# Tile pools that wait for their own bytes: reuse_waits="tile" on every SBUF and PSUM pool of a four-layer kernel

## The chip, the cores and the metric

The kernel runs on one core of one Trainium2 chip, as one launch. The metric is the device time in microseconds (us). Engines are named as in the profile: PE (matmul; PEld is its weight load), DVE (vector), ACT (scalar), POOL (GpSimd), SP (a queue that only issues DMAs here). A "q" after an engine's name, as in SPq, marks its instruction queue where DMAs are issued.

## The reference: what is computed

The input x is an image of 256 by 256 pixels with 128 channels, fp32. Four layers follow, each with a residual sum and each ahead with a group norm `gn` over 32 groups of channels:

```python
x = x + L0(gn(x))   # attention along the rows, 4 heads of 32, pair bias from x, sigmoid gate, projection
x = x + L1(gn(x))   # a, b = sigmoid((xWa1+ba1)*(xWa2+ba2)), ...; z = einsum('bikc,bkjc->bijc', a, b), 16 channels
                    # g * (LN(z) @ Wz + bz), g = sigmoid(x @ Wg + bg)
x = x + L2(gn(x))   # z = LN(x); a, b = sigmoid(z@Wg)*(z@Wl); k = einsum('bimc,bmjc->bijc', a, b), 128 channels
                    # sigmoid(z@Wgo+bgo) * (LN(k) @ Wlo + blo)
x = x + L3(gn(x))   # a 1x9 convolution to one channel with relu, added down the rows, twice;
                    # then a 1x1 product with relu, added along the columns, twice
```

A group norm needs the mean and variance of the whole image before the next layer can use any pixel. That is why the kernel is a chain of stages with a full statistic between most of them.

## The kernel before, in words

The image is held as 128 channels on the partitions by 65536 pixels. A slab is 2048 pixels (8 KB on each partition, 1 MB in all); there are 32. The image does not fit in SBUF, so each stage streams slabs from DRAM and stores slabs back: xT is the image before layer 0 in that layout, x1T, x2T and x3T are the images after layers 0, 1 and 2.

Stages, with the names of their tile pools and the time of each in the profiled span:

- **p0, p1** (0 to 246 us): load, transpose, statistics of the input; then row factors and pair bias.
- **p2** (246 to 1488): attention, in 64 groups of 4 image rows. The pools are `p2e` (the exponentials, e and es), `p2c` and `p2`. Per group SP loads x and the row factors; ACT centres (L509); PE projects and scores; the reciprocal sums rz go to DRAM and come back spread as rb (L618, L621), POOL multiplies (L636), PE projects (L643), DVE adds to x, and x is stored to x1T (L651). The last two groups store through ACT's queue.
- **chk**: a check that the scores stayed in range, from the statistics `gn_mv` (L799 to L809): chk_ok, a matmul, chk_bad, flag. The flag is read into registers and a conditional block (L811) computes the attention another way if it is set; it isn't in this run. After the block come the norm's factors (L199 to L210) and folded weights (L834 to L842).
- **p3** (1509 to 1582): 13 slab slots, each a pool of its own (`x1_0` to `x1_12`, 8 KB each). The first eight loads (L794 in `load1`) stand in the program ahead of the check. Products a and b go to DRAM (abD).
- **z** (1586 to 1650): the product over k for 16 channels, its norm, result to znD.
- **p4** (1645 to 1817): for each slab a gate on PE and ACT (L987, L990), z's product (L1014), DVE multiplies, POOL adds to x (L1035; DVE does it for six slabs), ACT sums squares (L997), SP stores the slab to x2T (L1041, last L1046), and SP loads later slabs into free slots. Small loads of z are issued by POOL (L973).
- **p5** (1825 to 2347): reads x2T into seven slab buffers (pool `x57`). The first four loads are issued by POOL, the others by SP (L1113). Column sums on PE (L1131) give mean and variance; ACT squares the mean into p5_m2 (L1137); then five products for each slab (L1174), and a and b to DRAM (aD, bD, L1224). The gates of the last two slabs come last.
- **p6** (2351 to 2643): 128 channel products; SP loads A and B (L1278, L1280), PE transposes (L1927) and multiplies (L1938); sums for the norm in k1 (DVE) and k2 (POOL).
- **p7** (2645 to 2916): normalises k, product, gate, residual, store to x3T.
- **p9** (2922 to 3281): layer 3: tap sums on PE (L1509), stored (L1521) and reloaded by image row, then the later relu steps and the output. It begins with a memset on POOL of the tile p9_S (L1695) and slab loads L1325, some of them on POOL's queue.

Memory is a stack of pools: a pool opened after another was released lands on the same bytes. In bytes per partition: the slots x1_0 to x1_12 stand at 48128 to 154624, and before them `p2e` at 48128 to 117760, `p2c` to 128000 and `p2` to 224256. The check's pool starts at 154624, `x57` at 40672, `p5` at 114400, p6 at 128736, p9 at 98016. PSUM is reused in the same way in its eight banks.

What sets the order of the work: within a block under `tc.manual_schedule()` (p0, p1, p2, p3, z, p4, p5, p6, p7 and p9 have one) every engine runs the instructions in the order in which the program gives them. Where such a block's instructions fall among those of its engine outside the block or in the next one is left to the library's planner, which reckons from when inputs and buffers are free. Each engine then runs its list strictly in order, and an instruction that waits holds those behind it. DMAs stand in the list of the engine that issues them.

Of the kernel before, what the change touches and what calls it, by code (L numbers as in the profile page):

```python
# [14 lines left out]
PSUM = bass.MemoryType.PSUM  # L15
# [17 lines left out]
def kernel(ctx: ExitStack, tc: tile.TileContext, a: dict, out: bass.AP):  # L33
# [36 lines left out]

    const = ctx.enter_context(tc.tile_pool(name="const", bufs=1))

# [120 lines left out]
    def gn_groups(mv, name):  # L193

        with tc.tile_pool(name=name + "_ps", bufs=1, space=PSUM) as ps, tc.tile_pool(
            name=name + "_sb", bufs=1
        ) as sb:
            pm = ps.tile([P, 1], F32, name=name + "_pm")
            nc.tensor.matmul(pm, lhsT=gmat, rhs=mv[:, 0:1], start=True, stop=True)  # L199
            mean = const.tile([P, 1], F32, name=name + "_mean")  # L200
            nc.vector.tensor_copy(mean, pm)
            d = sb.tile([P, 1], F32, name=name + "_d")
            nc.vector.tensor_sub(d, mv[:, 0:1], mean)
            nc.vector.scalar_tensor_tensor(d, d, d, mv[:, 1:2], ALU.mult, ALU.add)
            pv = ps.tile([P, 1], F32, name=name + "_pv")
            nc.tensor.matmul(pv, lhsT=gmat, rhs=d, start=True, stop=True)
            sd = sb.tile([P, 1], F32, name=name + "_sd")
            nc.scalar.activation(sd, pv, AF.Sqrt, bias=epst)
            rstd = const.tile([P, 1], F32, name=name + "_rstd")
            nc.vector.reciprocal(rstd, sd)  # L210
        return mean, rstd

    stats_pool = ctx.enter_context(tc.tile_pool(name="stats", bufs=2))

# [11 lines left out]
    layer0 = ExitStack()  # L226
    l0 = layer0.enter_context(tc.tile_pool(name="l0", bufs=1))
    mbT = l0.tile([P, 2, N], F32, name="mbT")
# [9 lines left out]
    RES = NSC // 2 + 2  # L238
    with tc.tile_pool(name="x0", bufs=1) as xres, tc.tile_pool(name="p0", bufs=3) as sb:
        held = {s: xres.tile([P, SC], F32, name=f"x0_{s}") for s in range(RES, NSC)}  # L240
        with tc.tile_pool(name="p0ps", bufs=3, space=PSUM) as ps, tc.tile_pool(
            name="f0ps", bufs=2, space=PSUM
        ) as fps, tc.tile_pool(name="f0", bufs=1) as wk, tc.manual_schedule():
            xts, loaded = {}, {}
# [164 lines left out]

        with tc.tile_pool(name="p1", bufs=2) as wk_sb, tc.tile_pool(  # L410
            name="p1ps", bufs=4, space=PSUM
        ) as ps, tc.tile_pool(name="p1pe", bufs=1, space=PSUM) as psE:

# [67 lines left out]
    qscale = 1.0 / float(HC) ** 0.5  # L481
    with tc.tile_pool(name="p2e", bufs=6) as eb, tc.tile_pool(name="p2c", bufs=1) as cs:
        triT = cs.tile([P, NH, 2, N], F32, name="triT")
        with tc.tile_pool(name="p2", bufs=2) as sb, tc.tile_pool(
            name="p2S", bufs=2, space=PSUM
        ) as psS, tc.tile_pool(name="p2z", bufs=1, space=PSUM) as psZ, tc.tile_pool(
            name="p2M", bufs=3, space=PSUM
        ) as psM, ExitStack() as by_hand:
            groups = {}
# [297 lines left out]
    SLOTS, FIRST = 13, 8  # L787
    x1_scope = ExitStack()
    slots = [x1_scope.enter_context(tc.tile_pool(name=f"x1_{i}", bufs=1)) for i in range(SLOTS)]
    xs = {}  # L790
# [10 lines left out]
    flag = const.tile([P, 1], mybir.dt.int32, name="flag")  # L801
    with tc.tile_pool(name="chk", bufs=1) as sb, tc.tile_pool(name="chkps", bufs=1, space=PSUM) as ps:
        ok = sb.tile([P, 2], F32, name="chk_ok")
        nc.vector.tensor_scalar(ok, mv1, 0.0, 0.0, ALU.mult, ALU.is_equal)
# [4 lines left out]
        nc.vector.tensor_tensor(flag, bad[:, 0:1], bad[:, 1:2], ALU.max)  # L809
# [21 lines left out]
    bgf = const.tile([P, 1], F32, name="bgf")  # L831
    with tc.tile_pool(name="f1ps", bufs=1, space=PSUM) as ps:
# [9 lines left out]
        nc.vector.tensor_tensor(bgf, bg1, pb, ALU.subtract)  # L842
# [6 lines left out]
    with x1_scope:  # L849
        with tc.tile_pool(name="p3", bufs=3) as sb, tc.tile_pool(  # L850
            name="p3ps", bufs=3, space=PSUM
        ) as ps, tc.manual_schedule():
            halves, done = [], []
# [37 lines left out]

        gate_pool = x1_scope.enter_context(tc.tile_pool(name="zg", bufs=3))
        with tc.tile_pool(name="z", bufs=2) as sb, tc.tile_pool(
            name="zps", bufs=3, space=PSUM
        ) as ps, tc.manual_schedule():
            Z = [gate_pool.tile([P, 4, 2 * N], F32, name="z_Z", tag="Z", bufs=4) for _ in range(4)]
# [201 lines left out]
    rs2_scope = ExitStack()  # L1098
    rs2_pool = rs2_scope.enter_context(tc.tile_pool(name="rs2", bufs=1))
# [3 lines left out]
    with tc.tile_pool(name="p5", bufs=2) as sb, tc.tile_pool(  # L1103
        name="p5q", bufs=4
    ) as sq_pool, tc.tile_pool(name="p5psX", bufs=1, space=PSUM) as psX, tc.tile_pool(
        name="p5psM", bufs=3, space=PSUM
    ) as psM, tc.manual_schedule():
        xs, sqs, zns, vars_ = {}, {}, {}, {}
# [691 lines left out]
def general_attention(tc, d, w, dram, stats1):  # L1800
# [6 lines left out]
    statD = dram.tile([N // G, P, 12], F32, name="statD")  # L1807
    with tc.tile_pool(name="gac", bufs=1) as cs, tc.tile_pool(name="ga", bufs=1) as sb, tc.tile_pool(
        name="gae", bufs=2
    ) as eb, tc.tile_pool(name="gaS", bufs=2, space=PSUM) as psS, tc.tile_pool(  # L1810
        name="gaT", bufs=2, space=PSUM
    ) as psT, tc.tile_pool(name="gaM", bufs=2, space=PSUM) as psM:
        tri = cs.tile([P, NH, 2, N], F32, name="ga_tri")
# [166 lines left out]
```

## Time and profile before

| | us |
|---|---|
| time, median of 3 runs | 3282.24 (3282.18 to 3283.38) |
| the profiled execution's own time | 3283.08 |
| its span | 3281.4 |
| PE busy | 3043.8 (93%) |
| DVE busy | 2246.1 (68%) |
| ACT busy | 2034.3 (62%) |
| POOL busy | 1773.0 (54%) |
| mean granted clock of PE | 0.963 |

By stage, busy PE: 1148.0 of 1148 us from 287 to 1435 (p2), 59.9 of 81 from 1509 to 1590 (p3), 137.3 of 140 from 1655 to 1795 (p4), 27.5 of 55 from 1795 to 1850 (p4 to p5), 484.9 of 487 from 1850 to 2337 (p5), 288.6 of 289 from 2354 to 2643 (p6), 247.1 of 248 from 2663 to 2911 (p7), 8.7 of 22 from 2911 to 2933 (p7 to p9).

A line of the timeline reads: start, busy time, engine, line of the program, operation, out<-in, shape, count, and in brackets the idle time of the engine before it and what ended that. A row of waits reads: who waited, for whom, us in total, times, longest. A row of the windows reads: the stretch, its length, busy us (count) of PE, PEld, DVE, ACT and POOL, granted clock, DMA share, GB/s.

### The profile page before, as it was taken

How to read it: one execution, taken by the hardware profiler on the slowest of the kernel's cores; microseconds unless marked ns; L12 is line 12 of the kernel's file. 1: busy time of each engine (PE TensorE's matmuls, PEld its weight loads, DVE VectorE, ACT ScalarE, POOL GpSimd, SP SyncE). 2: the span in 40 equal slices, each digit the busy share in tenths (PEclk: the TensorE clock that was granted, in tenths of full speed). 3: DMA queues.
4: the chain of work that ended last, by engine and by line, in shares of the span. 5: the costliest groups of instructions: out<-in, count | busy, mean ns of one | idle time of the engine just before them, and what ended most of it. 6: DMA issues, size and time to landing. Idle time of an engine off the chain costs nothing. (4 is left out here: it accounts for less than half of the span.)

```text
span 3281.4 us, 51765 instructions
## 1 busy us (share of the span) xinstructions
PE 3043.8 (93%) x19792; PEld 1631.1 (50%) x19792; DVE 2246.1 (68%) x2540; ACT 2034.3 (62%) x2270; POOL 1773.0 (54%) x1019
## 2 busy tenths in 40 slices
PE   5678999999999999996699699999999999979998
PEld 4524555555555555552433244444599943324444
DVE  5626888888888888883456445445455578868887
ACT  3576777777777777763467545444344457757776
POOL 4054777777777777770267100000155568858887
PEclk8898999999999999998999799999999999989999
DMA  9982333333333333329679667766699989986775
GB/s 355 368 325 90 119 117 107 122 111 111 118 111 113 120 107 121 114 88 394 232 299 398 264 232 302 290 226 264 245 351 351 353 321 389 388 304 193 233 232 153
DMA packets 294802, 749.18 MB, mean 228 GB/s; under 512 B 71127, under 2 KB 142185, under 8 KB 245369
## 3 DMA queue, kind: packets, MB, share of 16 engines
q1 hardware_dynamic: 282671, 731.12, 61.2%
q0 software_dynamic: 9040, 13.17, 1.2%
q8 instruction: 158, 2.59, 0.3%
q10 hardware_dynamic: 2840, 1.54, 0.2%
q14 instruction: 93, 0.76, 0.1%
HBM read 458.07 MB, written 287.64 MB: 227 GB/s over the span
## 5 line engine op out<-in xcount | busy, mean ns | idle before, releaser
L565 DVE TENSOR_TENSOR p_e<-p_S,triT 128x1024 f32<-128x1024 f32 x512 | 609.4, 1212 | 145.0 <-PE p_S L555 145.0
L575 POOL TENSOR_TENSOR p_es<-p_e 128x1024 f32<-128x1024 f32 x256 | 603.5, 2369 | 126.9 <-issue 66.1
L573 ACT ACTIVATE p_e<-p_e,mbT 128x1024 f32<-128x1024 f32 x512 | 551.9, 1138 | 62.9 <-DVE p_e L565 62.9
L1174 PE MATMUL p_pm<-p_zn,wf 128*128 128x512 f32 x1040 | 449.0, 593 | 2.1 <-ACT p_a L1209 1.9
L540 PE MATMUL p_mm<-p_xn,w 128*128 128x512 f32 x768 | 407.0, 613 | 0.3 <-DVE p_v L535 0.3
L1174 PEld LDWEIGHTS p_pm<-p_zn,wf 128*128 128x128 f32 x1040 | 197.1, 190 | 254.0 <-issue 246.4
L555 PE MATMUL p_S<-p_q,p_k 32*128 32x256 f32 x4096 | 296.4, 402 | 3.2 <-DVE p_e L565 3.2
L1271 POOL MEMSET k<- 128x512 f32 x1 | 0.5, 524 | 529.4 <-PE p_pm L1174 529.4
L555 PEld LDWEIGHTS p_S<-p_q,p_k 32*128 32x128 f32 x4096 | 186.7, 185 | 159.2 <-PE p_mm L531 91.6
L514 POOL TENSOR_TENSOR p_xn<-p_xn,p_rs 128x1024 f32<-128x1024 f32 x63 | 151.0, 2396 | 207.4 <-ACT p_xn L509 134.2
L1938 PE MATMUL tp_z<-p_B,tp_at 128*128 128x256 f32 x1024 | 250.7, 388 | 0.8 <-DMA p_B<-bD 0.5
L588 PE MATMUL p_o<-p_e,p_v 128*32 128x256 f32 x4096 | 249.3, 384 | 0.0
L1302 POOL TENSOR_TENSOR k<-k,p_sq 128x512 f32<-128x512 f32 x128 | 163.0, 1274 | 135.4 <-ACT p_sq L1300 135.4
L1938 PEld LDWEIGHTS tp_z<-p_B,tp_at 128*128 128x128 f32 x1024 | 185.5, 191 | 22.1 <-DVE tp_at L1929 1.6
L540 PEld LDWEIGHTS p_mm<-p_xn,w 128*128 128x128 f32 x768 | 126.8, 192 | 105.3 <-issue 89.6
L1301 DVE TENSOR_TENSOR k<-tp_z,k 128x512 f32<-128x512 f32 x128 | 88.6, 692 | 127.1 <-ACT p_sq L1300 127.1
L588 PEld LDWEIGHTS p_o<-p_e,p_v 128*32 128x32 f32 x4096 | 120.7, 110 | 110.1 <-ACT p_g L546 41.3
L1298 ACT COPY p_K<-tp_z 128x512 f32<-128x512 f32 x128 | 74.9, 585 | 157.7 <-PE tp_z L1938 157.7
L546 ACT ACTIVATE p_g<-p_mm,bgh 128x512 f32<-128x512 f32 x128 | 88.0, 687 | 131.4 <-PE p_mm L540 131.3
L1213 DVE SCALAR_TENSOR_TENSOR p_b<-p_pm,b2w,p_b 128x1024 f32<-128x1024 f32 x64 | 82.2, 1284 | 123.3 <-PE p_pm L1174 108.9
L544 ACT ACTIVATE p_k<-p_mm,cqkg 128x512 f32<-128x512 f32 x128 | 87.9, 687 | 125.2 <-PE p_mm L540 124.9
L531 PEld LDWEIGHTS p_mm<-w,p_xn 128*128 128x128 f32 x1024 | 134.4, 192 | 61.0 <-issue 60.5
(386 smaller groups left out, 6097.0 us busy)
## 6 DMA issues: line engine op xcount, KB each, us to landing
p_x<-x2T SPq DMA_DIRECT2D x60, 1024.0 KB
x<-x1T SPq DMA_DIRECT2D x51, 1024.0 KB
p_x<-in_x_dram SPq DMA_DIRECT2D x32, 1024.0 KB
p_x<-xT SPq DMA_DIRECT2D x64, 512.0 KB
x2T<-x SPq DMA_DIRECT2D x32, 1024.0 KB
aD<-p_a SPq DMA_DIRECT2D x32, 1024.0 KB
bD<-p_b SPq DMA_DIRECT2D x32, 1024.0 KB
p_A<-aD SPq DMA_DIRECT2D x32, 1024.0 KB
```

The costliest lines, as they stand in the source:

```text
L514: nc.gpsimd.tensor_tensor(xn, xn, groups[g]["rs"], ALU.mult)
L531: nc.tensor.matmul(pm[:, k * D : (k + 1) * D], lhsT=t["xn"][:, b * P : (b + 1) * P], rhs=wf[:, 2 * D : 3 * D], start=True, stop=True,)
L540: nc.tensor.matmul(pm, lhsT=w, rhs=t["xn"][:, cs_], start=True, stop=True)
L555: nc.tensor.matmul(Ss[h // 2][:, h % 2, u, :], lhsT=t["k"][hp, r * N + u * P : r * N + (u + 1) * P], rhs=t["q"][hp, r * N : (r + 1) * N], ...
L565: nc.vector.tensor_tensor(e[:, :, 2 * p : 2 * p + 2, :].rearrange("p u h n -> p h u n"), Ss[p], triT[:, 2 * p : 2 * p + 2, :, :], ALU.add,)
L573: nc.scalar.activation(e[:, u, :, :], e[:, u, :, :], AF.Exp, bias=mbT[:, u, i : i + 1])
L575: nc.gpsimd.tensor_tensor(es, e[:, 0, :, :], e[:, 1, :, :], ALU.add)
L588: nc.tensor.matmul(t["o"][hp, r % 2, :], lhsT=t["v"][:, r * 2 + u, hp], rhs=e[:, u, h, :], start=(u == 0), stop=(u == 1),)
L1174: nc.tensor.matmul(pm[:, c, :], lhsT=wf2[:, i, :], rhs=zns[s][:, k * CK : (k + 1) * CK], start=True, stop=True)
L1301: nc.vector.tensor_tensor(k1, pz, k1, ALU.add)
L1302: nc.gpsimd.tensor_tensor(k2, k2, sq, ALU.add)
L1938: nc.tensor.matmul(pz[:, t, :], lhsT=at[:, u, t * P : (t + 1) * P], rhs=Bc[:, u, :], start=(u == 0), stop=(u == 1))
```

## The change

Each `tc.tile_pool(...)` in SBUF and PSUM gets the argument `reuse_waits="tile"`. Nothing else differs: the same tiles, instructions and transfers, in the same program. The argument tells the library what a tile must wait for when its pool lies on bytes that released pools used. With the default, `"pool"`, every tile of the new pool waits for all users of all those older pools. With `"tile"`, a tile waits for the users of those older tiles that lie on its own bytes (in PSUM, in its own bank). Where the library can't follow an older pool's users it keeps the default for that pool. The waits are made by the library, so no line of the program shows them. A cut of the diff, which repeats for all pools:

```diff
-    with tc.tile_pool(name="p2e", bufs=6) as eb, tc.tile_pool(name="p2c", bufs=1) as cs:
+    with tc.tile_pool(name="p2e", bufs=6, reuse_waits="tile") as eb, tc.tile_pool(name="p2c", bufs=1, reuse_waits="tile") as cs:
...
-    slots = [x1_scope.enter_context(tc.tile_pool(name=f"x1_{i}", bufs=1)) for i in range(SLOTS)]
+    slots = [x1_scope.enter_context(tc.tile_pool(name=f"x1_{i}", bufs=1, reuse_waits="tile")) for i in range(SLOTS)]
...
-    with tc.tile_pool(name="chk", bufs=1) as sb, tc.tile_pool(name="chkps", bufs=1, space=PSUM) as ps:
+    with tc.tile_pool(name="chk", bufs=1, reuse_waits="tile") as sb, tc.tile_pool(name="chkps", bufs=1, space=PSUM, reuse_waits="tile") as ps:
...
-    x_pool = x_scope.enter_context(tc.tile_pool(name="x57", bufs=7))
+    x_pool = x_scope.enter_context(tc.tile_pool(name="x57", bufs=7, reuse_waits="tile"))
...
-    with tc.tile_pool(name="p6", bufs=3) as sb, tc.tile_pool(name="p6ps", bufs=3, space=PSUM) as ps:
+    with tc.tile_pool(name="p6", bufs=3, reuse_waits="tile") as sb, tc.tile_pool(name="p6ps", bufs=3, space=PSUM, reuse_waits="tile") as ps:
```

More of the change, by code (lines that the diff above doesn't have):

```diff
@@ L69 @@
     eD = dram.tile([1, N * NP], F32, name="eD")
-    const = ctx.enter_context(tc.tile_pool(name="const", bufs=1))
+    const = ctx.enter_context(tc.tile_pool(name="const", bufs=1, reuse_waits="tile"))
     ident = const.tile([P, P], F32, name="ident")
@@ L193, in gn_groups @@
     def gn_groups(mv, name):
-        with tc.tile_pool(name=name + "_ps", bufs=1, space=PSUM) as ps, tc.tile_pool(
-            name=name + "_sb", bufs=1
-        ) as sb:
+        with tc.tile_pool(name=name + "_ps", bufs=1, space=PSUM, reuse_waits="tile") as ps, tc.tile_pool(name=name + "_sb", bufs=1, reuse_waits="tile") as sb:
             pm = ps.tile([P, 1], F32, name=name + "_pm")
@@ L211, in gn_groups @@
         return mean, rstd
-    stats_pool = ctx.enter_context(tc.tile_pool(name="stats", bufs=2))
+    stats_pool = ctx.enter_context(tc.tile_pool(name="stats", bufs=2, reuse_waits="tile"))
     def new_stats(name):
@@ L226 @@
     layer0 = ExitStack()
-    l0 = layer0.enter_context(tc.tile_pool(name="l0", bufs=1))
+    l0 = layer0.enter_context(tc.tile_pool(name="l0", bufs=1, reuse_waits="tile"))
     mbT = l0.tile([P, 2, N], F32, name="mbT")
@@ L238 @@
     RES = NSC // 2 + 2
-    with tc.tile_pool(name="x0", bufs=1) as xres, tc.tile_pool(name="p0", bufs=3) as sb:
+    with tc.tile_pool(name="x0", bufs=1, reuse_waits="tile") as xres, tc.tile_pool(name="p0", bufs=3, reuse_waits="tile") as sb:
         held = {s: xres.tile([P, SC], F32, name=f"x0_{s}") for s in range(RES, NSC)}
-        with tc.tile_pool(name="p0ps", bufs=3, space=PSUM) as ps, tc.tile_pool(
-            name="f0ps", bufs=2, space=PSUM
-        ) as fps, tc.tile_pool(name="f0", bufs=1) as wk, tc.manual_schedule():
+        with tc.tile_pool(name="p0ps", bufs=3, space=PSUM, reuse_waits="tile") as ps, tc.tile_pool(name="f0ps", bufs=2, space=PSUM, reuse_waits="tile") as fps, tc.tile_pool(name="f0", bufs=1, reuse_waits="tile") as wk, tc.manual_schedule():
             xts, loaded = {}, {}
@@ L407 @@
         nc.vector.tensor_scalar(woh, wo, 0.5 * SHIFT, None, ALU.mult)
-        with tc.tile_pool(name="p1", bufs=2) as wk_sb, tc.tile_pool(
-            name="p1ps", bufs=4, space=PSUM
-        ) as ps, tc.tile_pool(name="p1pe", bufs=1, space=PSUM) as psE:
+        with tc.tile_pool(name="p1", bufs=2, reuse_waits="tile") as wk_sb, tc.tile_pool(name="p1ps", bufs=4, space=PSUM, reuse_waits="tile") as ps, tc.tile_pool(name="p1pe", bufs=1, space=PSUM, reuse_waits="tile") as psE:
             mw = wk_sb.tile([P, 32], F32, name="p1_mw", bufs=1)
@@ L481 @@
     qscale = 1.0 / float(HC) ** 0.5
-    with tc.tile_pool(name="p2e", bufs=6) as eb, tc.tile_pool(name="p2c", bufs=1) as cs:
+    with tc.tile_pool(name="p2e", bufs=6, reuse_waits="tile") as eb, tc.tile_pool(name="p2c", bufs=1, reuse_waits="tile") as cs:
         triT = cs.tile([P, NH, 2, N], F32, name="triT")
[L484 to L488, printed above, removed]
+        with tc.tile_pool(name="p2", bufs=2, reuse_waits="tile") as sb, tc.tile_pool(name="p2S", bufs=2, space=PSUM, reuse_waits="tile") as psS, tc.tile_pool(name="p2z", bufs=1, space=PSUM, reuse_waits="tile") as psZ, tc.tile_pool(name="p2M", bufs=3, space=PSUM, reuse_waits="tile") as psM, ExitStack() as by_hand:
             groups = {}
@@ L831 @@
     bgf = const.tile([P, 1], F32, name="bgf")
-    with tc.tile_pool(name="f1ps", bufs=1, space=PSUM) as ps:
+    with tc.tile_pool(name="f1ps", bufs=1, space=PSUM, reuse_waits="tile") as ps:
         for w, wf_, ub, vb, n in ((u1, v1, ub1, vb1, "1"), (u2, v2, ub2, vb2, "2")):
@@ L849 @@
     with x1_scope:
-        with tc.tile_pool(name="p3", bufs=3) as sb, tc.tile_pool(
-            name="p3ps", bufs=3, space=PSUM
-        ) as ps, tc.manual_schedule():
+        with tc.tile_pool(name="p3", bufs=3, reuse_waits="tile") as sb, tc.tile_pool(name="p3ps", bufs=3, space=PSUM, reuse_waits="tile") as ps, tc.manual_schedule():
             halves, done = [], []
@@ L888 @@
                 store3()
[L892 to L895, printed above, removed]
+        gate_pool = x1_scope.enter_context(tc.tile_pool(name="zg", bufs=3, reuse_waits="tile"))
+        with tc.tile_pool(name="z", bufs=2, reuse_waits="tile") as sb, tc.tile_pool(name="zps", bufs=3, space=PSUM, reuse_waits="tile") as ps, tc.manual_schedule():
             Z = [gate_pool.tile([P, 4, 2 * N], F32, name="z_Z", tag="Z", bufs=4) for _ in range(4)]
@@ L955 @@
                 nc.sync.dma_start(znD[4 * q : 4 * q + 4, :].rearrange("c (p t) -> p c t", p=P), zq)
-        with tc.tile_pool(name="p4", bufs=3) as sb, tc.tile_pool(
-            name="p4psg", bufs=2, space=PSUM
-        ) as psg, tc.tile_pool(name="p4psz", bufs=2, space=PSUM) as psz, tc.manual_schedule():
+        with tc.tile_pool(name="p4", bufs=3, reuse_waits="tile") as sb, tc.tile_pool(name="p4psg", bufs=2, space=PSUM, reuse_waits="tile") as psg, tc.tile_pool(name="p4psz", bufs=2, space=PSUM, reuse_waits="tile") as psz, tc.manual_schedule():
             zs, gts, sums = {}, {}, []
@@ L1072 @@
     off2 = const.tile([P, 1], F32, name="off2")
-    with tc.tile_pool(name="f2", bufs=1) as sb, tc.tile_pool(name="f2ps", bufs=1, space=PSUM) as ps:
+    with tc.tile_pool(name="f2", bufs=1, reuse_waits="tile") as sb, tc.tile_pool(name="f2ps", bufs=1, space=PSUM, reuse_waits="tile") as ps:
         po = ps.tile([P, 1], F32, name="f2_o")
@@ L1098 @@
     rs2_scope = ExitStack()
-    rs2_pool = rs2_scope.enter_context(tc.tile_pool(name="rs2", bufs=1))
+    rs2_pool = rs2_scope.enter_context(tc.tile_pool(name="rs2", bufs=1, reuse_waits="tile"))
     gates = {s: rs2_pool.tile([P, SC], F32, name=f"gate_{s}") for s in (NSC - 2, NSC - 1)}
@@ L1102 @@
     BT = KB * SC
[L1103 to L1107, printed above, removed]
+    with tc.tile_pool(name="p5", bufs=2, reuse_waits="tile") as sb, tc.tile_pool(name="p5q", bufs=4, reuse_waits="tile") as sq_pool, tc.tile_pool(name="p5psX", bufs=1, space=PSUM, reuse_waits="tile") as psX, tc.tile_pool(name="p5psM", bufs=3, space=PSUM, reuse_waits="tile") as psM, tc.manual_schedule():
         xs, sqs, zns, vars_ = {}, {}, {}, {}
@@ L1246 @@
     nc.vector.tensor_scalar(inside[:, NP // 8 :], inside[:, NP // 8 :], in_col, None, ALU.subtract)
-    rk_pool = rs2_scope.enter_context(tc.tile_pool(name="rk", bufs=1))
+    rk_pool = rs2_scope.enter_context(tc.tile_pool(name="rk", bufs=1, reuse_waits="tile"))
     rk = rk_pool.tile([P, CK], F32, name="rk")
@@ L1328 @@
     g2 = const.tile([P, NSC + 1], F32, name="g2")
-    with tc.tile_pool(name="p7", bufs=2) as sb, tc.tile_pool(name="p7psX", bufs=2, space=PSUM) as psX, tc.tile_pool(
-        name="p7psM", bufs=2, space=PSUM
-    ) as psM, tc.manual_schedule():
+    with tc.tile_pool(name="p7", bufs=2, reuse_waits="tile") as sb, tc.tile_pool(name="p7psX", bufs=2, space=PSUM, reuse_waits="tile") as psX, tc.tile_pool(name="p7psM", bufs=2, space=PSUM, reuse_waits="tile") as psM, tc.manual_schedule():
         ks, rks, rbs, gts = {}, {}, {}, dict(gates)
@@ L1477 @@
     k0 = const.tile([P, 1], F32, name="k0")
-    with tc.tile_pool(name="f3ps", bufs=1, space=PSUM) as ps:
+    with tc.tile_pool(name="f3ps", bufs=1, space=PSUM, reuse_waits="tile") as ps:
         pb = ps.tile([P, 1], F32, name="f3_s")
@@ L1497 @@
     LEAD = 6
-    with tc.tile_pool(name="p9", bufs=2) as sb, tc.tile_pool(name="p9psM", bufs=2, space=PSUM) as psM, tc.tile_pool(
-        name="p9psX", bufs=2, space=PSUM
-    ) as psX, tc.manual_schedule():
+    with tc.tile_pool(name="p9", bufs=2, reuse_waits="tile") as sb, tc.tile_pool(name="p9psM", bufs=2, space=PSUM, reuse_waits="tile") as psM, tc.tile_pool(name="p9psX", bufs=2, space=PSUM, reuse_waits="tile") as psX, tc.manual_schedule():
         xs, zs, pbs, qs, blocks = xs9, {}, {}, {}, {}
@@ L1807, in general_attention @@
     statD = dram.tile([N // G, P, 12], F32, name="statD")
[L1808 to L1812, printed above, removed]
+    with tc.tile_pool(name="gac", bufs=1, reuse_waits="tile") as cs, tc.tile_pool(name="ga", bufs=1, reuse_waits="tile") as sb, tc.tile_pool(name="gae", bufs=2, reuse_waits="tile") as eb, tc.tile_pool(name="gaS", bufs=2, space=PSUM, reuse_waits="tile") as psS, tc.tile_pool(name="gaT", bufs=2, space=PSUM, reuse_waits="tile") as psT, tc.tile_pool(name="gaM", bufs=2, space=PSUM, reuse_waits="tile") as psM:
         tri = cs.tile([P, NH, 2, N], F32, name="ga_tri")
```

## The prediction

> **What bounds the kernel now.** I read the page first, then busy time by stage, then for each boundary between two stages the timeline, the waits of the engines and of the DMA queues, and last the bytes on which each stage's tiles lie. Times are microseconds from the span's start.
>
> ```profile
> PE 3043.8 (93%) x19792; PEld 1631.1 (50%) x19792; DVE 2246.1 (68%) x2540; ACT 2034.3 (62%) x2270; POOL 1773.0 (54%) x1019
> PE   5678999999999999996699699999999999979998
> 1498.00:1502.00 4.00, 0.00 (x0) 0.00 (x0) 0.15 (x1) 1.28 (x1) 0.00 (x0) 0.50 0.55 158
> 1510.00:1576.00 66.00, 57.71 (x504) 15.49 (x500) 21.78 (x29) 35.37 (x57) 0.00 (x0) 0.96 1.01 408
> ```
>
> PE is busy 93%. The two window rows give PE, its loads, DVE, ACT and POOL, then granted clock, DMA share and GB/s. The second (stage p3) has PE busy 57.7 of 66 us and the DMA share at 1.01: p3 is set by DMA. In p2 (287 to 1435), p5 (1850 to 2337), p6 and p7 PE has work without a gap, and no wait on a pool can be taken out of that. What the change can move lies in the boundaries, so the sum is made there. PE has no work for some 238 us of the span, in stages bound by DMA as well as at boundaries.
>
> **What the change adds.** No compute instruction and no transfer: only waits go, and where a later stage's load can start earlier the planner may place it earlier in its engine's queue. So the cost side is queue order: what is queued behind a load that waits on SP or POOL.
>
> **p0 to p1, p3 to z.** The waits that end these are data (DVE's means; the stores of a and b, then their loads, which PE waits 13.4 us for). 0; an earlier p3 end passes through.
>
> **p1 to p2.** ACT centres group 0 at 250.11, waiting for a load that SP issued at 246.29 behind a pool wait, and L468 behind it runs at 251.17 though DVE was ready at 249.72: at most 1.4 gained. An earlier 0.5 MB load competes with p1's transfers: at 373 GB/s, 1.4 lost. I take +0.8.
>
> **p2 to p3.** Timeline, then SP's waits:
>
> ```profile
> 1486.96 0.35 ACTq L651 DMA_DIRECT2D x1T<-p_x  x1
> 1488.59 0.16 DVE L190 SCALAR_TENSOR_TENSOR gn_mv<-gn_b,gn_mv_d 128x1 f32<-128x1 f32 x1
> 1494.99 0.17 DVE L804 TENSOR_SCALAR chk_ok<-gn_mv 128x2 f32<-128x2 f32 x1 [6.24 <-DMA x<-x1T]
> 1496.05 0.16 DVE L809 TENSOR_TENSOR flag<-chk_bad 128x1 int32<-128x1 f32 x1
> 1500.32 2.60 SPq L794 DMA_DIRECT2D x<-x1T  x5
> 1509.51 2.79 PE L872 MATMUL p<-x,v 128*32 128x512 f32 x12 [0.25 <-DVE bgf L842]
> ```
> ```profile
> SPq L794 <- PE p_z L598: 3.1, 1, 3.1
> ```
>
> chk_ok reads only gn_mv, ready at 1488.75, yet starts at 1494.99: its pool stands on bytes of p2's pool, whose last users are the x1T stores issued until 1486.96. Its own bytes belonged to a normalised input read long before, so the 6.24 go, and flag comes at about 1489.8. Late next: the branch. On its skipped side SP waits until the transfers of all earlier loads and stores have landed, 1497.6 to 1500.2, and only then issues the other five loads (1500.32). That is the hole of the 1498 to 1502 window. These transfers are the first eight 1 MB loads, from 1474.77, held 3.1 us by the last sums of p2 (PE p_z); tile by tile all but one of the slots are free by 1472.6. If SP keeps its order, loads begin at 1471.2 + 0.4 = 1471.6 and finish 3.2 earlier; if the planner moves them ahead of the last groups' small transfers, up to 11 earlier, but then rz and rb of group 62 (SP, 1466.34 to 1469.4; POOL's L636 and PE's output wait for rb) queue behind megabytes and lose up to 6. As p3 is DMA-bound to its last load, the gain is how much earlier the loads start plus the hole closed: 3.0 at least, 8.7 at most (1500.3 back to about 1491.6, flag's chain with the same 1.8 to the branch). I take +6.4, two thirds up, as the chk wait is sure and the hoist is not; 0 if the hoist's loss comes with it.
>
> **z to p4.** Gates' PSUM banks come free 0.8 earlier; an earlier sigmoid on ACT can push the square root at 1635.95 back by a table load (1.28). −0.3 to +1.8; +0.4.
>
> **p4 to p5.** POOL's and ACT's timelines, and the tile view of the x2T stores:
>
> ```profile
> 1801.84 0.59 POOL L1113 DMA_DIRECT2D p_x<-x2T  x1 [7.14 <-DMA x2T<-x]
> 1802.45 4.53 POOL L1035 TENSOR_TENSOR x<-x,p_g 128x2048 f32<-128x2048 f32 x1
> 1807.01 2.00 ACT L997 ACTIVATE p_junk<-x,c1neg 128x2048 f32<-128x2048 f32 x1 [8.09 <-POOL x L1035]
> ...
> 1832.81 0.69 ACT L1137 ACTIVATE p_m<-p_st,off 128x512 f32<-128x512 f32 x1 [6.23 <-DMA x2T<-x]
> ```
> ```profile
> DMA to landing us min/median/max: 5.3/11.4/13.8
> ```
>
> Two stalls. (b) ACT's square into p5_m2 has its input at 1829.24 (PE's last column sum) and waits until 1832.81 for the last x2T store, from a tile on other bytes. Its own bytes were a tile stored at 1807. So 1832.81 − 1829.24 = +3.57, and the factor chain behind it to the first dense product stretch at 1847 moves along. (a) POOL's first p5 load stands in its queue ahead of an add and holds it 7.14 us, waiting for store 25; ACT's statistics behind come up to 4.9 late. With tile waits that load depends on an early slot (store 19, issued 1760.40) and may be placed mid-p4, right after add 20 (ends 1765.1). It then waits for the store to land; the second load's slots still hang on stores 24 and 25, so the 7.14 may simply be the second load's.
> Here a rule and the row differ. The Trainium skill (DMA: Bandwidth & Descriptors, section "Anatomy of one DMA — SWDGE (gpsimd) path") gives a transfer about 2.0 us plus bytes over 436 GB/s: an estimate of 4.4 for 1 MB, so store 19 has landed by 1764.8 and POOL waits for nothing. The row says 11.4 from issue to landing at a DMA share of 0.9 in p4: landed at 1771.8, POOL stalled about 1771.8 − 1765.1 − 1.2 (the two z loads there) = 5.5. PE repeats its 4.7 us step there with ACT nearly as full; POOL's 4.29 us gap four adds on takes up most, not all, of it. So (a) lies between −8.1 (the stall in mid-p4, plus 2.6 for 1 MB of an SP load ahead of the late stores at 400 GB/s) and +4.9 (gone). By the rule (a) would be 0 and this boundary +3.6, the sum 15; I take the measured row, and with the gap (a) = −3.1, between the 1.2 left after it and the 5.5 without it. p4 to p5: 3.57 − 3.1 = +0.5, ends −4.5 and +8.5.
>
> **p5 to p6.** SP's waits, then the timeline:
>
> ```profile
> SPq L1278 <- DMA bD<-p_b: 3.4, 1, 3.4
> SPq L1278 <- PE p_pm L1174: 1.1, 1, 1.1
> ```
> ```profile
> 2346.87 0.33 SPq L1278 DMA_DIRECT2D p_A<-aD  x1
> 2351.62 1.96 PE L1927 MATMUL tp_a<-ident,p_A 128*128 128x128 f32 x8 [4.83 <-DMA p_A<-aD]
> ```
>
> The first A load waits until 2346.84, the gates' last product (pool wait). Its data, aD, were in place at about 2342.0 and its bytes (a normalised tile of slab 29) long before; B's data, bD, at 2345.8 against an issue at 2347.26. A then lands before PE's last gate at 2346.8; transposes start at about 2347.0, and PE next waits for B: 2345.8 in place of 2347.26 is 1.5 earlier for certain, the transposes take 1.96 + copy 1.2 out of the way. First product from 2354.11 to about 2350.6: +3.5 (3 to 4.5); p6 is PE-bound from there and keeps it. Without that cover (A's bytes under a late tile) 1.5.
>
> **p6 to p7.** The chain k1/k2, rkD store and load, L1089 is data. A broadcast on POOL freed of its 3.65 us wait could go before the last k2 add: −0.7 to 0; −0.3.
>
> **p7 to p9.**
>
> ```profile
> 2921.11 0.65 POOL L1695 MEMSET p_S<- 128x666 f32 x1 [9.43 <-issue]
> ```
>
> The memset waits for a tile of the norm (2921.0); freed, two 1 MB loads behind it start near 2916, before the tap stores that they now meet in the queues (ACT waits 2.42 for one, DVE 10.09 for the taps). 0 to 2.5; +0.7.
>
> **Sum.** 0.8 + 6.4 + 0.4 + 0.5 + 3.5 − 0.3 + 0.7 = 12.0. The profiled run took 3283.1 (span 3281.4 and 1.7 around it), so 3271.1; against the median 3282.24, 0.8 lower, **3270**.
>
> **Rivals.** 0.2%, 6.6 us, is about what a measurement of this kernel can tell from no change.
> (1) Larger: loads climb far enough and POOL's stall dissolves too: p2 to p3 8.7 (+2.3), p4 to p5 8.5 (+8): 22.3, **3260**. For it: store 25's landing is the only thing that holds POOL. Against: 1.0 DMA share there.
> (2) Smaller: SP's loads start only 3.2 earlier (3.0), p5 to p6 3, p4 to p5 −2: 4, **3278**. For it: rb's queue on SP.
> (3) Slower: p5's loads on POOL each move up behind the add whose store they wait for; each costs 11.4 − 4.5 = 6.9, three of them 20.7 in a stage where PE has no slack, against the other 11.5: 9 worse, **3291**. It decides once p4 loses 11.5 (level) or 18 (measurable). Against: POOL's 4.29 gap, and slots whose stores are long gone.
> (4) The planner can't follow the users through the conditional block and keeps whole pools: **3282**. For it: the branch between p2 and p3; against: p5, p6 and p9 lie clear of it.
>
> **How the numbers follow.** The forecast 55% (own range 3264 to 3276), (1) 25%, (2) 10%, (3) 5%, (4) 5%. The range 3257 to 3279 leaves out (3), (4), a third of (2), and the low quarter of (1). Faster: 54 + 25 + 3 = 82%; same: 1 + 7 + 5 = 13%; slower 5%.
>
> **What would show it.** chk_ok within 0.3 us of gn_mv; first x1T loads before 1472, no DMA hole at the branch, p3's last load 3 to 9 earlier; ACT's p_m directly after PE's p_st; an A load before the last gates; POOL's memset near 2914. For (a): where POOL's p5 loads stand and the idle before them. It is wrong if rz or rb of group 62 lands late, if p4's adds come more than 5 us late, or if any dense stretch of PE (p2, p5, p6, p7) changes its length by over 2 us.

## The result, and the profile after

The changed kernel takes 3269.64 us (median of 6 runs, 3266.57 to 3273.64) against 3282.8 (6 runs), a ratio of 0.9961 with a 95% interval of 0.9948 to 0.9974. A second series gave 0.9968 (0.9956 to 0.9980). That is 10 to 13 us faster, near the 12 forecast, but most of the steps came out at other sizes than those in the sum.

In the traces every engine runs the same instructions in the same order before and after; only the waits differ. So a difference below is a wait that went, what happened because it went, or the scatter between executions. The profile's line numbers fall by 10 to 28 (p3's loads are L784 for L794, chk_ok L794 for L804, POOL's broadcast L1331 for L1353, the sum and max of k2 L1381 and L1382 for L1403 and L1404).

From p2 to p3, timeline of the changed kernel (start, busy us, instruction):

```profile
1467.17 40.73 SPq L784 DMA_DIRECT2D x<-x1T  x17
1485.62 0.16 DVE L190 SCALAR_TENSOR_TENSOR gn_mv<-gn_b,gn_mv_d 128x1 f32<-128x1 f32 x1
1485.81 0.17 DVE L794 TENSOR_SCALAR chk_ok<-gn_mv 128x2 f32<-128x2 f32 x1
1486.86 0.16 DVE L799 TENSOR_TENSOR flag<-chk_bad 128x1 int32<-128x1 f32 x1
1495.20 12.70 SPq L784 DMA_DIRECT2D x<-x1T  x9
1498.28 13.95 PE L860 MATMUL p<-x,v 128*32 128x512 f32 x108
```

SP's waits there: in the branch (after), and for the products whose slots later loads take (of before from 1500 to 1530, then of after from 1495 to 1525). Then windows (columns as before: PE, PEld, DVE, ACT, POOL, granted clock, DMA share, GB/s):

```profile
SPq L801 <- SPq L801: 6.7, 3, 5.5
...
SPq L794 <- PE p L872: 17.4, 7, 10.2
...
SPq L784 <- PE p L860: 8.9, 5, 3.7
```
```profile
1492.00:1496.00 4.00, 0.64 (x3) 0.61 (x3) 0.69 (x4) 0.85 (x1) 0.00 (x0) 0.50 0.10 33
1496.00:1562.00 66.00, 55.25 (x484) 15.75 (x484) 21.49 (x34) 33.39 (x55) 0.00 (x0) 0.95 1.01 412
1511.00:1525.00 14.00, 14.00 (x116) 3.75 (x112) 4.80 (x7) 9.16 (x14) 0.00 (x0) 0.85 0.99 365
1506.00:1520.00 14.00, 14.00 (x136) 3.96 (x132) 6.36 (x9) 10.55 (x18) 0.00 (x0) 1.00 1.01 409
```

chk_ok follows gn_mv at once: the 6.24 us are gone. But between the flag (1486.86) and the next load (1495.20) SP stands 6.7 us in the branch, L801, until the earlier transfers have landed, and the DMA engines then have a hole with a share of 0.10. The hole has moved and deepened (before, the share was 0.55 over 4 us), not closed. After it p3 is DMA-bound as before. What also changed is the start of p3: the fourteenth load takes the slot that p3's first products free, and as these came 28.1 us after p2's last sum in place of 34.8, SP's longest wait for them fell from 10.2 to 3.7. Over 14 us from there the transfers ran at 409 GB/s in place of 365 (last two rows, of before and of after).

From p4 to p5, POOL's and ACT's timelines:

```profile
1786.43 0.59 POOL L1093 DMA_DIRECT2D p_x<-x2T  x1
1787.03 4.55 POOL L1019 TENSOR_TENSOR x<-x,p_g 128x2048 f32<-128x2048 f32 x1
1796.95 1.09 POOL L1093 DMA_DIRECT2D p_x<-x2T  x2 [5.36 <-DMA x2T<-x]
...
1819.34 0.69 ACT L1117 ACTIVATE p_m<-p_st,off 128x512 f32<-128x512 f32 x1 [2.73 <-PE p_st L1111]
```

POOL's first p5 load stands where it stood, between the same two adds, and no longer waits; the second waits 5.36. ACT's p_m follows PE's column sum at once: it starts 0.1 after that sum's end, where it started 3.6 after it before.

From p5 to p6, PE's first product of before, which the prediction did not show, and then the rows of after:

```profile
2354.11 3.75 PE L1938 MATMUL tp_z<-p_B,tp_at 128*128 128x256 f32 x8 [0.54 <-DMA p_B<-bD]
```
```profile
2328.90 0.33 SPq L1258 DMA_DIRECT2D p_A<-aD  x1
2332.94 0.33 SPq L1260 DMA_DIRECT2D p_B<-bD  x1
2335.88 1.98 PE L1899 MATMUL tp_a<-ident,p_A 128*128 128x128 f32 x8 [2.56 <-DMA p_A<-aD]
2338.47 3.75 PE L1910 MATMUL tp_z<-p_B,tp_at 128*128 128x256 f32 x8 [0.61 <-DMA p_B<-bD]
```

The first A load is issued 4.4 before PE's last gate product (it was issued at that product's end), but took 7.0 to reach PE's transpose, where it took 4.75 before. The first product waits for B in both. B is issued 0.4 before the last gate product's end, where it was issued 0.5 after it, and PE starts on it 5.5 after the issue in place of 6.9.

From p6 to p7, the rows of before, which the prediction did not show, and then those of after:

```profile
2646.55 0.69 DVE L1403 TENSOR_TENSOR k<-k,k 128x512 f32<-128x512 f32 x1
2647.28 0.43 DVE L1404 TENSOR_SCALAR k<-k 128x512 f32<-128x512 f32 x1
2649.54 4.49 POOL L1353 PARTITION_BROADCAST p_rb<-rs__17911  x2 [3.65 <-DMA kD<-p_K]
```
```profile
2630.14 5.27 POOL L1331 PARTITION_BROADCAST p_rb<-rs__17911  x2
2630.78 2.47 DVE L1381 TENSOR_TENSOR k<-k,k 128x512 f32<-128x512 f32 x1
2633.28 2.40 DVE L1382 TENSOR_SCALAR k<-k 128x512 f32<-128x512 f32 x1
```

POOL's broadcasts lost their wait and now run beside DVE's sum and max of k2. These two took 1.12 together and now take 4.87. Here the change loses time.

From p7 to p9, ACT's root of the norm, of before and of after:

```profile
2916.58 1.28 ACT L208 ACT_TABLE_LOAD   x1
2920.55 0.26 ACT L208 ACTIVATE gn_sd<-gn_pv,epst 128x1 f32<-128x1 f32 x1 [2.69 <-PE gn_pv L206]
```
```profile
2908.39 1.28 ACT L206 ACT_TABLE_LOAD   x1 [4.18 <-PE gn_pv L204]
2909.69 0.26 ACT L206 ACTIVATE gn_sd<-gn_pv,epst 128x1 f32<-128x1 f32 x1
```

The table load used to run while ACT waited for PE. In the trace of before, three waits for DMAs stand ahead of it; after, these are gone, the load stands behind the wait for PE and lies on the chain. That the number of waits sets its place is inferred.

To place the gain I measured pieces between fixed instructions, which a shift of everything before does not touch. "As before" are the profiles of the kernel before and of p7_alone (below), which differ only in p7; "changed" are two profiles of the changed kernel.

| piece, us | as before | changed | difference of means |
|---|---|---|---|
| span's start to p2's last sum | 1474.7, 1469.0 | 1470.2, 1469.7 | within the spread |
| to p3's last product | 102.8, 102.3 | 100.3, 99.8 | −2.5 |
| first transpose of z to p4's last product | 219.3, 219.3 | 218.1, 217.7 | −1.4 |
| to the last square sum | 11.7, 12.3 | 10.0, 9.5 | −2.2 |
| to p_m | 11.0, 11.8 | 7.5, 7.5 | −3.9 |
| p5's last product to the last k2 sum | 299.1, 299.7 | 296.8, 296.8 | −2.6 |
| to the product that spreads rk | 17.1 (before alone) | 20.5, 20.7 | +3.5 |
| to p7's last product | 248.3, 248.3 | 248.6, 248.6 | +0.3 |
| to the first tap sum | 10.8, 10.8 | 11.4, 11.4 | +0.6 |
| to the end | 359.3, 361.3 | 361.1, 362.7 | within the spread |

The differences add up to −8.2. The timed ratios say −13 and −11, with intervals that begin at −8.5 and −6.6; the rest would lie in the start and in p9, whose pieces vary by more than that between kernels that share them (p9: 359 to 368). The p4 pieces are soft too: over the seven profiles of kernels with these pools there, POOL's wait for a store is 3.2 to 7.7 (5.4 above), the piece to p4's last product 217.7 to 224.8, and the piece to the last square sum 7.8 to 10.0. The others repeat within 1.0, with one exception explained below (check and slots together).

### The profile page after: what moved, and what is told of

It reads as the page before. It is cut to its first block, busy times and chain, and to the rows that moved or that the text cites. A ratio compares the mean times of both kernels' runs of the same rounds, so it can differ in the third digit from the quotient of the medians.

```text
span 3271.7 us, 51718 instructions
## 1 busy us (share of the span) xinstructions
PE 3040.7 (93%) x19792; PEld 1629.4 (50%) x19792; DVE 2248.5 (69%) x2540; ACT 2033.8 (62%) x2270; POOL 1773.4 (54%) x1019
## 5 line engine op out<-in xcount | busy, mean ns | idle before, releaser
L578 PE MATMUL p_o<-p_e,p_v 128*32 128x256 f32 x4096 | 248.6, 383 | 0.0
```

The source lines that it names most:

```text
L578: nc.tensor.matmul(t["o"][hp, r % 2, :], lhsT=t["v"][:, r * 2 + u, hp], rhs=e[:, u, h, :], start=(u == 0), stop=(u == 1),)
```

## Experiments

Every kernel is the one before with the argument on chosen pools, and edits as shown. The cuts write the argument out; in the runs a helper sets it by the pool's name. Where a text says "as all_but_p7", all pools but p7's three have it.

**p7's pools alone.**

```diff
-    with tc.tile_pool(name="p7", bufs=2) as sb, tc.tile_pool(name="p7psX", bufs=2, space=PSUM) as psX, tc.tile_pool(
-        name="p7psM", bufs=2, space=PSUM
+    with tc.tile_pool(name="p7", bufs=2, reuse_waits="tile") as sb, tc.tile_pool(name="p7psX", bufs=2, space=PSUM, reuse_waits="tile") as psX, tc.tile_pool(
+        name="p7psM", bufs=2, space=PSUM, reuse_waits="tile"
```

> Only stage p7's three pools wait tile by tile, all others as before. Theory (the changed kernel lost some 3.5 us between p6 and p7 because POOL's two broadcasts now start at once and hold DVE's sum and max of k2, 0.69 and 0.43 us, for 2.4 us each): the same two DVE rows take about 2.4 each, PE's third gate product comes 3 to 4 us later against the last product of p6, and the time is about 3.5 us above before (ratio 1.0011). Rival (the loss came with the earlier shift of other stages or with their transfers): both rows as before, no change of time (1.0000).

Measured: ratio 1.0011 (1.0003 to 1.0019, 22 runs), which is +3.6 us. Timeline of this kernel:

```profile
2642.07 5.26 POOL L1353 PARTITION_BROADCAST p_rb<-rs__17911  x2
2642.70 2.47 DVE L1403 TENSOR_TENSOR k<-k,k 128x512 f32<-128x512 f32 x1
2645.20 2.40 DVE L1404 TENSOR_SCALAR k<-k 128x512 f32<-128x512 f32 x1
```

The same two rows, and 20.8 in place of 17.1 from the last k2 sum to the spread of rk. So this part of the change by itself makes the kernel slower, by about as much as the DVE rows grow (3.75; the interval is 1 to 6 us).

**Everything but p7.** The cut is against the changed kernel.

```diff
-    with tc.tile_pool(name="p7", bufs=2, reuse_waits="tile") as sb, tc.tile_pool(name="p7psX", bufs=2, space=PSUM, reuse_waits="tile") as psX, tc.tile_pool(name="p7psM", bufs=2, space=PSUM, reuse_waits="tile") as psM, tc.manual_schedule():
+    with tc.tile_pool(name="p7", bufs=2) as sb, tc.tile_pool(name="p7psX", bufs=2, space=PSUM) as psX, tc.tile_pool(name="p7psM", bufs=2, space=PSUM) as psM, tc.manual_schedule():
```

> All pools tile by tile except p7's three. Theory: the two DVE rows are 0.69 and 0.43 again, POOL's broadcasts wait about 3.6 for the store of K, and the time is 3.5 below the changed kernel's, about 3266 (ratio to before 0.995). Rival: the loss stays, 3269.6 (0.9961).

Measured: ratio 0.9953 (0.9940 to 0.9966); 17.1 from k2 to rk again.

```profile
2623.56 0.69 DVE L1403 TENSOR_TENSOR k<-k,k 128x512 f32<-128x512 f32 x1
2624.29 0.43 DVE L1404 TENSOR_SCALAR k<-k 128x512 f32<-128x512 f32 x1
2625.50 3.35 DVE L1406 RECIPROCAL k<-k 128x512 f32<-128x512 f32 x1 [0.79 <-ACT k L1405]
2626.53 4.49 POOL L1353 PARTITION_BROADCAST p_rb<-rs__17911  x2 [3.61 <-DMA kD<-p_K]
```

In the profile the loss is gone. The timed gain over the changed kernel is of the expected sign, but the intervals overlap. The reciprocal, with one input, runs beside a broadcast and both keep their times (3.35, and 4.49 for two).

**Another form for the sum and the max,** with the argument on all pools.

```diff
-        nc.vector.tensor_tensor(k2, k2, k1, ALU.add)
-        nc.vector.tensor_scalar(k2, k2, 0.0, None, ALU.max)
+        nc.vector.scalar_tensor_tensor(k2, k2, 1.0, k1, ALU.mult, ALU.add)
+        nc.vector.scalar_tensor_tensor(k2, k2, 0.0, k2, ALU.max, ALU.max)
```

> All pools tile by tile, and the sum and the max of k2 written as two DVE instructions of the scalar_tensor_tensor form (k2*1+k1, then max(k2,0) max k2). Theory (POOL's broadcast holds only the fast forms of DVE, as the scalar_tensor_tensor of k1 beside it kept its 1.20): 1.2 each beside the broadcasts, 2.4 in place of 4.9, so 2.5 below the changed kernel (3267, ratio 0.9953). Rival (any DVE instruction on SBUF is held beside a broadcast): 2.4 or more each and no gain (0.9961).

Measured: 0.9961 (0.9947 to 0.9975), and

```profile
2623.26 2.46 DVE L1403 SCALAR_TENSOR_TENSOR k<-k,k 128x512 f32<-128x512 f32 x1
2625.75 2.53 DVE L1404 SCALAR_TENSOR_TENSOR k<-k 128x512 f32<-128x512 f32 x1
```

My theory fell: this form, 1.20 when no broadcast runs ahead of it, is held as long as the others. The k1 row, which had kept its 1.20, began before the broadcast.

**The max on ACT,** with the argument on all pools.

```diff
-        nc.vector.tensor_scalar(k2, k2, 0.0, None, ALU.max)
+        nc.scalar.activation(k2, k2, AF.Relu)
```

> All pools tile by tile; the max of k2 with zero on ACT in place of DVE. Theory (held beside POOL's broadcast are DVE instructions with two SBUF inputs and the fast one-input form, not others): the sum still takes 2.4, the reciprocal, one input, runs its 3.35 though the second broadcast is still under way, and the spread of rk comes 1 to 2 earlier than in the changed kernel (19 from the last k2 sum in place of 20.5). Rival (any DVE instruction on SBUF alone is held): the reciprocal takes up to 1 longer and the gain is gone.

Measured: 3271.74 (one run), 20.2 from k2 to rk against 20.5. Inconclusive: ACT needed another table load (1.28) after the Relu, so the reciprocal began at 2633.73, after the second broadcast had ended at 2633.16, and met nothing.

**Nine loads ahead of the branch.**

```diff
-    SLOTS, FIRST = 13, 8
+    SLOTS, FIRST = 13, 9
```

> As all_but_p7, with nine x1T loads ahead of the check's branch in place of eight. Theory (the DMA engines stand idle about 4 us at the branch because the eight loads have landed before SP may issue more, and p3 is bound by DMA): a ninth MB fills 2.4 of it, p3 ends 2 us earlier, 3264 (0.9944). Rival (SP's later landing wait moves by the same 2.4): the same as all_but_p7 (0.995).

Measured: 0.9951 (0.9936 to 0.9966), 99.9 us to p3's last product as in all_but_p7 (99.8). Windows:

```profile
1492.00:1496.00 4.00, 0.56 (x2) 0.50 (x2) 0.31 (x2) 0.00 (x0) 0.00 (x0) 0.50 0.83 330
1496.00:1500.00 4.00, 2.59 (x28) 1.82 (x32) 1.58 (x9) 0.26 (x1) 0.00 (x0) 0.50 0.30 68
```

The rival held: one more load moves the hole back by its own length. The first load behind the branch comes 27.0 after p2's last sum, against 24.6 in all_but_p7, so the transfers under way must land before SP goes on.

**The check and p5's pools** (p5 has four; one is cut here).

```diff
-    with tc.tile_pool(name="chk", bufs=1) as sb, tc.tile_pool(name="chkps", bufs=1, space=PSUM) as ps:
+    with tc.tile_pool(name="chk", bufs=1, reuse_waits="tile") as sb, tc.tile_pool(name="chkps", bufs=1, space=PSUM, reuse_waits="tile") as ps:
...
-    with tc.tile_pool(name="p5", bufs=2) as sb, tc.tile_pool(
+    with tc.tile_pool(name="p5", bufs=2, reuse_waits="tile") as sb, tc.tile_pool(
```

> Tile by tile only the check's two pools and stage p5's four. Theory: chk_ok runs right after gn_mv (6 us sooner after it), but p3's end does not move, since the loads start as before and SP still waits for all eight to land: from p2's last sum to p3's last product 102.5 us as before (changed kernel 100.3). Rival of the prediction (the check's wait is on the path): 98 or less. At p5: from the last square sum to ACT's p_m 7.5 in place of 11.0, and POOL's 7 us wait ahead of its first p5 load stays.

Measured: 3278.56 (one run). To p3's last product 102.8, no gain, though chk_ok follows gn_mv by 0.2 and p3's first product comes 4 earlier. SP's longest wait for p3's products falls to 4.1, but the loads start no earlier and the first load behind the branch comes 27.3 after p2's last sum, in place of 25.7; why the earlier ones landed that late is open. From the last square sum to p_m 7.5. POOL's first load waits 7.04.

**Slots, p5's buffers and p6** (with the pool rk).

```diff
-    slots = [x1_scope.enter_context(tc.tile_pool(name=f"x1_{i}", bufs=1)) for i in range(SLOTS)]
+    slots = [x1_scope.enter_context(tc.tile_pool(name=f"x1_{i}", bufs=1, reuse_waits="tile")) for i in range(SLOTS)]
...
-    x_pool = x_scope.enter_context(tc.tile_pool(name="x57", bufs=7))
+    x_pool = x_scope.enter_context(tc.tile_pool(name="x57", bufs=7, reuse_waits="tile"))
...
-    rk_pool = rs2_scope.enter_context(tc.tile_pool(name="rk", bufs=1))
+    rk_pool = rs2_scope.enter_context(tc.tile_pool(name="rk", bufs=1, reuse_waits="tile"))
...
-    with tc.tile_pool(name="p6", bufs=3) as sb, tc.tile_pool(name="p6ps", bufs=3, space=PSUM) as ps:
+    with tc.tile_pool(name="p6", bufs=3, reuse_waits="tile") as sb, tc.tile_pool(name="p6ps", bufs=3, space=PSUM, reuse_waits="tile") as ps:
```

> Tile by tile only the thirteen slab slots, the seven p5 buffers, and stage p6's pools with rk. Theory: the loads start 3 us earlier against p2's last sum and this alone brings p3's end 2.5 earlier (100.0 from the last sum); chk_ok still waits for the stores of x1T, hidden. Rival: without the check's part nothing or half of it. POOL's p5 wait moves one add later and falls from 7 to 3 to 5, the last square sum comes 2 to 4 earlier after p4's last product (8 to 10 in place of 12). ACT's p_m still waits for the last store. From p5's last product to the last k2 sum 296.4 in place of 299.4. Sum of these 8 to 9 less what p_m gives back.

Measured: 3277.45 (one run). To p3's last product 102.4: no gain either, against my theory. The loads began 3 earlier against p2's last sum, but

```profile
1490.18 0.17 DVE L804 TENSOR_SCALAR chk_ok<-gn_mv 128x2 f32<-128x2 f32 x1 [6.11 <-DMA x1T<-p_x]
```

now the check's wait was the late one. SP's waits and a window from the start of p3 on:

```profile
SPq L794 <- PE p L872: 17.1, 8, 9.7
...
1505.00:1519.00 14.00, 14.00 (x120) 3.75 (x116) 5.25 (x7) 9.39 (x15) 0.00 (x0) 0.89 0.98 366
```

The first load behind the branch came 25.0 after p2's last sum, as in the changed kernel. But p3's first product came at 34.3, so SP again waited 9.7 for a slot, and the transfers ran at 366 GB/s there, where the changed kernel had 409. To the last square sum 7.3 (POOL waited 2.64), p_m still waited 6.16 for the store, and from p5's last product to the last k2 sum 296.5.

**The check and the slots together.**

```diff
-    slots = [x1_scope.enter_context(tc.tile_pool(name=f"x1_{i}", bufs=1)) for i in range(SLOTS)]
+    slots = [x1_scope.enter_context(tc.tile_pool(name=f"x1_{i}", bufs=1, reuse_waits="tile")) for i in range(SLOTS)]
...
-    with tc.tile_pool(name="chk", bufs=1) as sb, tc.tile_pool(name="chkps", bufs=1, space=PSUM) as ps:
+    with tc.tile_pool(name="chk", bufs=1, reuse_waits="tile") as sb, tc.tile_pool(name="chkps", bufs=1, space=PSUM, reuse_waits="tile") as ps:
```

> Tile by tile only the check's two pools and the thirteen slots. Theory (both waits end together: the branch needs the flag and the landed loads, and either alone left p3's end where it was): from p2's last sum to p3's last product 100, p3's first product at 28. Rival (other pools, p3's own or PSUM's, made the gain): 102.5. From there on everything as before: 11 to p_m, 299 to the last k2 sum, 17 to the spread of rk.

Measured: 3278.26 (one run). 100.0 to p3's last product, 28.2 to its first: the whole gain, with no other pool. SP's waits and a window as above:

```profile
SPq L794 <- PE p L872: 11.0, 8, 4.2
...
1505.00:1519.00 14.00, 14.00 (x136) 3.86 (x132) 6.50 (x9) 10.35 (x18) 0.00 (x0) 1.00 1.01 421
```

p_m 11.9, k2 300.0, as before. From k2 to rk 14.4, where nothing was changed. The cause is PE's clock. Windows over the gate products in that piece, of before and of this kernel:

```profile
2653.00:2659.00 6.00, 5.78 (x7) 2.50 (x8) 2.64 (x3) 2.87 (x3) 3.33 (x2) 0.52 0.67 270
2646.00:2652.00 6.00, 5.90 (x14) 2.68 (x15) 4.18 (x5) 4.28 (x4) 3.92 (x3) 1.00 0.65 262
```

At a granted clock of 0.52 PE did 7 products in 6 us, at 1.00 it did 14. In this execution the low clock (0.53 over 3.5 us) fell on the eight products before these, behind which PE waits anyhow.

**POOL's wait in p4's tail: loads on ACT, and a root ahead of time.**

```diff
-                (nc.gpsimd if s < KB else nc.sync).dma_start(xs[s], x2T[:, s * SC : (s + 1) * SC])
+                (nc.gpsimd if s < 1 else nc.scalar if s < KB else nc.sync).dma_start(xs[s], x2T[:, s * SC : (s + 1) * SC])
...
             load7x(s + 5) if s + 5 < NSC else load9(s + 5 - NSC)
+        nc.scalar.activation(const.tile([P, 1], F32, name="warm"), epst, AF.Sqrt)
```

> As all_but_p7; p5's loads 1 to 3 issued by ACT in place of POOL, and one square root of a constant column on ACT at the end of p7, so that the table is loaded before the norm's root. Theory: POOL's last adds run without a wait (3.2 and three issues of 0.55 less) while ACT waits anyhow: last square sum 4 earlier; the table load (1.28) leaves the chain p7 to p9: together 5, 3262 (ratio 0.9937). Rival (ACT's load holds the last gate, which POOL and DVE then wait for): nothing at p4, 1.3 at p9: 3266 (0.995).

Measured: 0.9963 (0.9949 to 0.9978). ACT's timeline:

```profile
1800.01 0.34 ACTq L1113 DMA_DIRECT2D p_x<-x2T  x1
1800.45 1.11 ACT L990 ACTIVATE p_g<-p_pg,bgf 128x1024 f32<-128x1024 f32 x1 [13.31 <-DVE x L1031]
```

The rival held: the load stands ahead of the last gate and waits for stores until 1800.01, so ACT is idle 13.3 us (the row names the gate's own last wait, which ended later still). The two p4 pieces took 230.0 together, against 227.0 in all_but_p7.

**Another order of p5's loads.**

```diff
-        for s in range(7):
+        for s in (0, 6, 1, 2, 3, 5, 4):
             load5(s)
...
             load7x(s + 5) if s + 5 < NSC else load9(s + 5 - NSC)
+        nc.scalar.activation(const.tile([P, 1], F32, name="warm"), epst, AF.Sqrt)
```

> As all_but_p7; p5's loads issued in the order 0, 6, 1, 2, 3, 5, 4, so that the three on POOL take buffers whose stores landed one store earlier, SP's load 6 taking the late one; and the square root of a constant at p7's end. Theory: POOL's 3.2 us wait in p4's tail goes, from p3's end on the last square sum comes 3 earlier than in all_but_p7, the chain p7 to p9 is 1.3 shorter: ratio 0.994 and 2 to 5 below the changed kernel. Rival (SP's load 6 waits for the late store in SP's queue and holds the last stores, or the adds are bound by DVE): p4 as in all_but_p7, 0.995.

Measured: 0.9956 (0.9941 to 0.9972). POOL still waited 3.56, and SP issued load 6 only at 1805.09, with the last stores behind it; no gain in p4. From p7's last product to the first tap sum 10.1.

**Everything but p7, with the root.**

```diff
             load7x(s + 5) if s + 5 < NSC else load9(s + 5 - NSC)
+        nc.scalar.activation(const.tile([P, 1], F32, name="warm"), epst, AF.Sqrt)
```

> As all_but_p7, with one square root of a constant column on ACT at the end of p7. Theory: p7's loss (3.4) and the table load that fell onto the norm's chain (1.3) are both gone: from p7's last product to the first tap sum 10.1 in place of 11.4, ratio 0.9945, some 4 below the changed kernel's 0.9965. Rival (p9 absorbs it): 0.9953.

Measured: 0.9954 (0.9941 to 0.9968). The table load is off the chain (10.1 in place of 11.4), but the time is that of all_but_p7: p4 took 224.8 in this profile (POOL's wait was 7.7), so a piece of 1.3 is not to be seen in the time.

**The changed kernel again**, beside best_two.

> The changed kernel once more, every pool tile by tile, beside the next one. Every theory: its first ratio, 0.996, and the same pieces: 100.2 us from p2's last sum to p3's last product, 7.5 from the last square sum to ACT's p_m, 296.5 from p5's last product to the last k2 sum, 20.5 from there to the product that spreads rk.

Measured: 0.9968 (0.9956 to 0.9980), 11 runs; its pieces are in the table.

No version is shown to be faster than the changed kernel: all_but_p7 is so in its profile, by 3.4 at one place, and its interval includes the changed kernel's ratio.

## Why the prediction was right, step by step

The total, 12.0, met the measured 11 to 13, and that is in part luck: errors of both signs cancelled, and of the measured gain 3 to 5 us lie in no piece of the table. What was right is that nothing but waits goes, that the gain lies at the boundaries, and that the dense stretches of PE keep their length (p5 499.6 us before and 499.2 after, p7 in the table).

- **A premise was wrong.** The text let the planner move loads up the queues, and the ends of the p2 to p3 and p4 to p5 steps and the slower rival came from that. No instruction moved. The rival with p5's loads climbing POOL's queue could not happen.
- **p2 to p3: +6.4 forecast, 2.5 measured.** The step "plus the hole closed" failed. By the text's own reading SP goes on only when the loads have landed, so loads that start 3.2 earlier open the branch 3.2 earlier; all above 3.0 rested on the hoist. In fact the loads started 3.1 earlier against p2's last sum, but SP went on only about 1 earlier (24.7 and 25.0, against 25.7 and 25.9). So most of the loads' lead was lost in the hole, and it is partly luck that 3.0 lies so near 2.5. The rest came from a wait that the text did not price: SP's wait for the slots that p3's first products free, which the earlier flag shortened. Also "the chk wait is sure" failed: taken alone it gave nothing (102.8), and the slots alone nothing (102.4). The gain needed both: earlier loads, and products early enough to free slots for the later ones.
- **p4 to p5: +0.5 forecast, about 6 measured.** (b), 3.57, was right: 3.9, and from p5's pools alone. (a) had the wrong sign, −3.1 against +2.2. The measured landing time used there still holds (median 11.6 in the changed kernel), but it was charged to a load in mid-p4. The load stayed where it was; the wait went to the second load, as the text allowed, and was shorter (5.4 for 7.1), as one more add ran ahead of it. By the Trainium skill's figure that the prediction cites, (a) was to be 0. That came nearer, though not by its reason: the section is on transfers that GpSimd issues, the store is SP's, and POOL did wait for a store.
- **p5 to p6: +3.5 forecast, 2.6 measured.** A's load did go ahead of the last gate products. Mis-sized were the landings. A took 7.0, not 4.75, beside the store of b that it now meets, and did not land before the last gate product. And B, which ended last, was given no landing time: it was issued 0.8 earlier against the last gate product (1.5 forecast), and with the 6.9 us from issue to product of before it gives a first product at 2352.7, not 2350.6. It took 5.5, and the first product came 2.2 earlier against the last gate product.
- **p6 to p7: −0.3 forecast, −3.5 measured.** The step named the broadcast that would run early, and priced only the POOL time in front of the k2 add. It did not ask what runs on DVE beside it.
- **p7 to p9: +0.7 forecast, −0.6 measured.** The memset did come early (2902.1, which is 7 earlier against p7's last product), but the tap sums did not gain, and the root's table load lost its cover.
- **p1 to p2 (+0.8) and z to p4 (+0.4)**: the first is not seen; the second may be up to 1.4, within what p4 varies.
- **Two sums** of the text are off, without effect: two thirds of the way from 3.0 to 8.7 is 6.8, and rival (2) leaves out the steps of +0.8, +0.4, −0.3 and +0.7, with which it would be 5.6.

## What to carry to other kernels

A wait that is taken away lets its instruction run sooner beside whatever is there: ask which engine it will meet, not only which it will release. Where two waits hold one stage, each in its own way, test them together, for each alone may show nothing. A branch that waits for every transfer under way puts a hole into a stage that is bound by transfers, and neither an earlier flag nor more loads ahead of it takes that away.

## What the runs showed of the hardware

A DVE instruction that starts while POOL's broadcast runs can be held to the broadcast's end. Held were a sum of two SBUF tiles (0.69 to 2.47), a scalar_tensor_tensor of two (1.20 to 2.46) and a tensor_scalar of one (0.43 to 2.40); the held ones ended 0.3 to 0.4 after a broadcast did, and the broadcasts grew from 2.30 to 2.70. Not held were the one-input reciprocal (3.35 beside one) and the gate products that read PSUM (1.28). The Trainium skill (SBUF — State Buffer, section "Who interferes with whom") says that DVE and GpSimd share a pair of SBUF ports, that a DVE instruction with two SBUF inputs contends for it with a GpSimd instruction that reads SBUF, that tensor_scalar can do so in its 2-port modes, and that the one that issues first has the pair for its whole instruction. These rows agree with it.

The waits of a branch that isn't taken cost as well: on SP 6.7 us in the changed kernel, with a DMA share of 0.10 from 1492 to 1496.
